# A graph-network layer on one core: rows of x fetched by SyncE and ScalarE's queue beside GpSimd's gathers, transfers moved to ScalarE's queue, copies moved to VectorE, shorter packing sums

## The chip, the cores and the metric

The kernel runs on one core of one Trainium2 chip. The metric is device time in microseconds (us); lower is better. A core has five engines that run side by side [...]: TensorE (PE, matrix products), VectorE (DVE), ScalarE (ACT), GpSimd (POOL) and SyncE (SP). SP, ACT and POOL each also have a queue from which they issue transfers (DMA) between the main memory (HBM) and the on-chip memory (SBUF); TensorE writes to a second on-chip memory, PSUM.

## The reference, cut to what matters

There are N = 50,000 nodes with D = 160 features and E = 1,650,000 edges (33 per node on average), sorted by destination; every node also has one edge from itself to itself.

```python
ss, vv = s[src], v[src]                       # one row of x per edge: the gather
out0 = C0 * (ss * e0 @ W1 + dot(vv, e1) * INV3 @ W2)
out1 = C1 * (p3 + p4 + p5)                    # all linear in x[src], scaled by the edge's 4 numbers
m_agg = segment_sum(concat(out0, out1), dst)  # sum over the edges of each node
h  = m_agg @ (Ws, Wv)                         # linear
x1 = layernorm(x + x + relu(h))
```

Everything before the relu is linear. So the kernel sums, for each node and each of the four edge numbers k, attr[e,k] * x[src[e]] over the node's edges, and applies one folded weight matrix per k afterwards.

## The kernel before, in words

**Units and groups.** The sorted edges are cut into units of 128 edges. Six units are a group (G = 6), and the destinations of a group lie within W = 32 consecutive nodes. There are 2,100 groups, taken two at a time (PG = 2) as a pair: 1,050 pairs of 12 units, 12,600 units in all. For a unit, GpSimd issues one indirect transfer (`gather`, L288) that reads 128 rows of x, 640 bytes each, into the tile `xg`, one per partition. VectorE builds the matrix `ha` (L297, L300) that puts each edge's four numbers in the columns of its destination; TensorE multiplies (`group_sums`, L325) and adds the six units of a group in PSUM. `xg` has six buffers (pool `rows`), `ha` three.

**Packing.** In the 1,980 middle groups a row is 787 edges long (L = 768 + 19), and self edges are taken out so that 768 remain. `pack` (L341) does this for 120 groups at once (17 packs): it loads source, destination and attributes (L351 to L354), marks the first 19 self edges of each row, sums their attributes by destination with 256 VectorE instructions (L389: 4 numbers, 32 destinations, two halves of the row), closes the gaps in steps of powers of two (L401 to L418), and stores the packed lists to HBM (L422, L423), from which `load` (L231) reads them back. The self edges' contribution is added when the group's sums leave PSUM (L334): it needs the 32 own rows of x, four times over, which `own` (L305) loads. For each pair `own` first reads two offsets from SBUF into SP's registers (L310) and then issues two transfers of 80 KB (L315); its pool has four buffers and it runs three pairs ahead.

**After the sums.** `turn` transposes the sums of two pairs (L436) and copies them out of PSUM (L439, the function `evict`), `apply_weights` multiplies by the folded weights (L450) and copies again (L454), `block` adds what belongs to 128 nodes (L480) and starts the layer norm, whose last step `norm3` (L188) stores the result (L192).

**Order.** The program is one long list, written by the loop over pairs at L595: load the next lists every ten pairs, gather, spread, sums, `own(p + 3)`, `fetch(p)`, some steps of `pack` (a generator; each `yield` is a place where it pauses, STEPS of them spread over the pairs), and then what `after_pair` has put off to this pair. Every engine and every queue works through its own instructions in that order. All loads and the packed stores are on SP's queue (`nc.sync`); the result's store is on ACT's (`nc.scalar`).

**The helper that is switched off.** `fetch` (L505), the plan of `batches` (L487 to L501) and the shortened `gather` (L287) can fetch whole units without GpSimd: an engine in `HELP` reads the offsets of some rows into registers (L510) and issues one transfer of 640 bytes for each row (L515). `HELP` (L63) is empty here, so none of it runs, and `evict` (L229) is ScalarE's copy.

Of the kernel before, what the change touches and what calls it, by code (L numbers as in the profile page):

```python
# [37 lines left out]
U8 = mybir.dt.uint8  # L38
# [24 lines left out]
HELP = {}  # L63
HEAD = 100
RP = 120
ROWS = 32
# [28 lines left out]
def tile_gnn_resnorm(ctx: ExitStack, tc: tile.TileContext, x, src, dst, attr, W1, W2, W3, W4, W5, Ws, Wv, out, n_edges):  # L95
# [92 lines left out]
    def norm3(pool, y, mv, rstd, n, row):  # L188
        nc.vector.reciprocal(rstd[:n], rstd[:n])  # L189
        o = pool.tile([P, D], F32, name="o")  # L190
        nc.vector.tensor_scalar(o[:n], y[:n], mv[:n, 0:1], rstd[:n], op0=ALU.subtract, op1=ALU.mult)  # L191
        nc.scalar.dma_start(out[row, :], o[:n])  # L192
# [18 lines left out]
    with tc.tile_pool(name="once", bufs=1) as once, tc.tile_pool(name="raw", bufs=2) as rawp, \  # L211
            tc.tile_pool(name="idx", bufs=2) as idxp, tc.tile_pool(name="rows", bufs=6) as rowp, \
            tc.tile_pool(name="far", bufs=3) as farp, tc.tile_pool(name="own", bufs=4) as ownp, \
# [13 lines left out]

        offsets = {}
        evict = nc.vector.tensor_copy if ET.Activation in HELP else nc.scalar.copy  # L229

        def load(s):  # L231
# [4 lines left out]
            if NH <= g0 < NH + NPK:  # L236
# [3 lines left out]
                for i in range(2):  # L240
                    nc.sync.dma_start(rf[:n, i, :], sd[i:i + 1, e].rearrange("o (u p) -> (o u) p", p=P))
                nc.sync.dma_start(ra[:n].rearrange("u p k -> u (p k)"), ad[e].rearrange("(u p) k -> u (p k)", p=P))
# [3 lines left out]
            nc.sync.dma_start(ri[:n, 0, :], src1[e].rearrange("(u p) o -> u (p o)", p=P))  # L246
            nc.sync.dma_start(ri[:n, 1, :], dst1[e].rearrange("(u p) o -> u (p o)", p=P))
            nc.sync.dma_start(ra[:n].rearrange("u p k -> u (p k)"), attr[e].rearrange("(u p) k -> u (p k)", p=P))
# [55 lines left out]

        def own(p):  # L305

            s, g, ng = pairs[p]
            if not NH <= g < NH + NPK:
                return
            _, at = nc.values_load_multi_w_load_instructions(  # L310
                baseO[0:1, g:g + ng], engines=[ET.SP], min_val=0, max_val=(N - W) * 4 * D,
                skip_runtime_bounds_check_because="an offset of a row of x")
            xo = ownp.tile([P, PG, D], F32, name="xo")
            for i, v in enumerate(at):
                nc.sync.dma_start(xo[:, i, :].bitcast(U8),  # L315
                                  xbytes[ds(v, W * 4 * D)].rearrange("(w f) -> w f", w=W).unsqueeze(0)
                                  .to_broadcast([NK, W, 4 * D]))
            owns[p] = xo
# [19 lines left out]
        owns, stored, taken = {}, {}, {}  # L338
        halves = ((0, L // 2), (L // 2, L))

        def pack(c):  # L341
# [9 lines left out]
            nc.sync.dma_start(pri[:n, 0, :], src1[e].rearrange("(r e) o -> r (e o)", e=L))  # L351
            nc.sync.dma_start(pri[:n, 1, :], dst1[e].rearrange("(r e) o -> r (e o)", e=L))
            nc.sync.dma_start(pra[:n].rearrange("r e k -> r (e k)"), attr[e].rearrange("(r e) k -> r (e k)", e=L))
            nc.sync.dma_start(pb[:n], base_d[NH + r0:NH + r0 + n])  # L354
            yield
            nc.scalar.copy(prs[:n], pri[:n])
# [3 lines left out]
            cum = packp.tile([P, L], F32, name="cum")  # L360
            far = packp.tile([P, L], I32, name="far")
            less = packp.tile([P, L], I32, name="less")
            carry = packp.tile([P, 1], F32, name="carry")
            pbf = packp.tile([P, 1], F32, name="pbf")
            mine = packp.tile([P, 2, NK * W], F32, name="mine")
            waste = packp.tile([P, L], BF16, name="waste")
            nc.vector.tensor_scalar(pbf[:n], pb[:n], float(N - W), None, op0=ALU.min)
            for h, (a, e) in enumerate(halves):
                q = slice(0, e - a)
                nc.vector.tensor_tensor(m[:, q], prs[:n, 0, a:e], prs[:n, 1, a:e], op=ALU.is_equal)  # L370
                nc.vector.tensor_tensor_scan(cum[:n, a:e], m[:, q], zeros[:n].to_broadcast([n, e - a]),
                                             carry[:n] if h else 0.0, op0=ALU.add, op1=ALU.add)
                nc.vector.tensor_copy(carry[:n], cum[:n, e - 1:e])
                yield

                nc.vector.scalar_tensor_tensor(m[:, q], cum[:n, a:e], float(K), m[:, q], op0=ALU.is_le, op1=ALU.mult)
                nc.vector.tensor_scalar(cum[:n, a:e], cum[:n, a:e], float(K), None, op0=ALU.min)
                nc.vector.scalar_tensor_tensor(far[:n, a:e], m[:, q], 0.0, cum[:n, a:e],
                                               op0=ALU.is_equal, op1=ALU.mult)
                yield  # L380
                nc.vector.tensor_scalar(cum[:n, a:e], prs[:n, 1, a:e], pbf[:n], None, op0=ALU.subtract)
                nc.vector.tensor_reduce(packed[:n, 0, 2 * c + h:2 * c + h + 1], cum[:n, a:e], axis=AX.X, op=ALU.min)
                nc.vector.tensor_reduce(packed[:n, 1, 2 * c + h:2 * c + h + 1], cum[:n, a:e], axis=AX.X, op=ALU.max)

                nc.vector.scalar_tensor_tensor(m[:, q], cum[:n, a:e], 1.0, m[:, q], op0=ALU.add, op1=ALU.mult)
                yield
                for k in range(NK):
                    for w in range(W):
                        nc.vector.scalar_tensor_tensor(waste[:n, a:e], m[:, q], float(w + 1), pra[:n, a:e, k],  # L389
                                                       op0=ALU.is_equal, op1=ALU.mult,  # L390
                                                       accum_out=mine[:n, h, k * W + w:k * W + w + 1])
                        if w % 4 == 3:
                            yield
            nc.vector.tensor_copy(counts[:n, c:c + 1], carry[:n])
# [426 lines left out]
```

## Time and profile before

| what | value |
|---|---|
| time, median of 3 runs | 18925.21 us (18899.5 to 18944.16) |
| the profiled execution's own time | 15879.8 us |
| its span, first to last instruction | 15878.0 us |
| GpSimd | 12,611 instructions, 75% of the span marked busy |
| TensorE products | 75% |
| VectorE | 50% |
| ScalarE | 6% |
| transfers, mean share of 16 DMA engines | about 0.3 in all slices |

The profile is of one execution. Its own time is 3045 us (16%) below the median of the timed runs, so durations from it are read as shares of its own span. "Busy" of GpSimd leaves out the time between two of its instructions, which is its own as well. SP's queue is not counted among the engines; what it issues is seen by asking for a line or for its waits.

### The profile page before, as it was taken

The page shows a single profiled execution, that of the slowest core. Times are in us where ns is not written, and L with a number is a line of the kernel's source. Part 1 is how long each engine was busy: PE and PEld are TensorE (multiplying, and loading weights), DVE is VectorE, ACT ScalarE, POOL GpSimd, SP SyncE. Part 2 cuts the span into 40 slices and gives each one's busy share as a digit, 9 for nine tenths or more (in the row PEclk, how much of TensorE's full clock was granted, in tenths as well). Part 3 has the DMA queues.
Part 4 walks back from the last instruction along what each step waited for, and adds up shares of the span by engine and source line. Part 5 has one row for each costly group of instructions (what it writes and reads, how often), then busy time and mean ns, then how long its engine had stood idle before and what let it go on. Part 6 is the DMA issues. An engine that isn't in the chain of part 4 may idle for free. (4 is left out here: it accounts for less than half of the span.)

```text
span 15878.0 us, 132047 instructions
## 1 busy us (share of the span) xinstructions
PE 11902.0 (75%) x43059; PEld 8781.1 (55%) x43060; DVE 7960.7 (50%) x17460; ACT 897.9 (6%) x2069; POOL 11926.1 (75%) x12611
## 2 busy tenths in 40 slices
PE   7677777777777777777777777777777777777777
PEld 4455555555555555555555555555555555555555
DVE  4565555545454554545454554545455454545422
ACT  0000000000000000000000000000000000000000
POOL 7677777777777777777777777777777777777776
PEclk7666666666666666666666666666666666666666
DMA  3333333333333333333333333333333333333332
GB/s 83 74 86 94 84 82 96 82 95 84 94 83 92 85 82 96 83 96 83 94 85 87 91 82 96 84 94 84 94 83 82 96 82 96 83 93 84 86 83 70
DMA packets 1040422, 1382.05 MB, mean 87 GB/s; under 512 B 233153, under 2 KB 813393, under 8 KB 1035641
## 3 DMA queue, kind: packets, MB, share of 16 engines
q0 software_dynamic: 604800, 1033.00, 26.9%
q1 hardware_dynamic: 378065, 307.98, 7.1%
q10 hardware_dynamic: 56864, 32.58, 0.7%
q8 instruction: 344, 5.64, 0.1%
q14 instruction: 349, 2.86, 0.1%
HBM read 1303.90 MB, written 68.75 MB: 86 GB/s over the span
## 5 line engine op out<-in xcount | busy, mean ns | idle before, releaser
L288 POOL DMA_INDIRECT xg<-in_x,si x12600 | 11924.5, 946 | 3917.0 <-issue 3527.0
L325 PE MATMUL ps<-xg,ha 128*128 128x160 f32 x25200 | 8037.7, 447 | 3686.5 <-DMA xg<-in_x,si 3640.6
L325 PEld LDWEIGHTS ps<-xg,ha 128*128 128x128 f32 x25200 | 5302.5, 266 | 6227.7 <-DMA xg<-in_x,si 6033.2
L334 DVE SCALAR_TENSOR_TENSOR A<-xo,taken,ps 128x160 f32<-128x160 f32 x1980 | 728.8, 377 | 7231.3 <-PE ps L325 7231.3
L389 DVE SCALAR_TENSOR_TENSOR waste<-marks,pra 120x393 bf16<-120x393 f32 (+3 forms) x4352 | 3652.5, 839 | 2.9
L300 DVE TENSOR_TENSOR ha<-hot,pk 128x1536 f32<-128x1536 f32 x1050 | 1830.2, 1744 | 284.1 <-PE ps L325 284.0
L480 PE MATMUL phb<-hp,hot 128*128 128x160 f32 x4544 | 1181.0, 433 | 56.2 <-ACT at L439 52.8
L480 PEld LDWEIGHTS phb<-hp,hot 128*128 128x128 f32 x4544 | 1066.4, 297 | 173.3 <-ACT at L439 172.2
L436 PE MATMUL pt<-ident,A 128*128 128x128 f32 (+1 forms) x4200 | 1051.7, 406 | 100.1 <-ACT hp L454 67.8
L450 PE MATMUL phc<-BWb,at 32*128 32x160 f32 x4200 | 1078.0, 404 | 0.0
L439 ACT COPY at<-pt 128x512 f32<-128x512 f32 (+1 forms) x1050 | 596.9, 579 | 6815.1 <-PE pt L436 6746.4
L450 PEld LDWEIGHTS phc<-BWb,at 32*128 32x128 f32 x4200 | 835.0, 253 | 196.3 <-issue 196.1
L450 PE MATMUL phc<-BWa,at 128*128 128x160 f32 x4200 | 922.6, 374 | 2.3 <-ACT at L439 2.0
L436 PEld LDWEIGHTS pt<-ident,A 128*128 128x128 f32 (+1 forms) x4200 | 700.7, 178 | 302.7 <-ACT hp L454 143.1
L450 PEld LDWEIGHTS phc<-BWa,at 128*128 128x128 f32 x4200 | 847.0, 255 | 35.3 <-ACT at L439 35.3
L297 DVE TENSOR_TENSOR hot<-bank,rel 128x384 f32<-128x384 f32 x1050 | 569.6, 544 | 0.3
L454 ACT COPY hp<-phc 128x160 f32<-128x160 f32 x525 | 153.3, 292 | 6230.2 <-PE phc L450 6171.5
L470 DVE TENSOR_TENSOR hot<-bank,rr 128x768 f32<-128x768 f32 (+2 forms) x391 | 358.8, 918 | 0.1
L389 DVE DVE_READ_ACCUMULATOR waste<-marks,pra 120x1 f32 (+1 forms) x4352 | 342.9, 79 | 0.0
L416 DVE COPY_PREDICATED pra<-marks,pra 120x1572 f32<-120x1572 int32 (+6 forms) x170 | 323.5, 1903 | 0.0
L176 DVE SCALAR_TENSOR_TENSOR y<-phb,xt 128x160 f32<-128x160 f32 x391 | 120.6, 308 | 195.6 <-PE phb L480 195.3
L414 DVE COPY_PREDICATED prs<-marks,prs 120x393 f32<-120x393 int32 (+6 forms) x340 | 181.3, 582 | 0.1
(98 smaller groups left out, 1610.1 us busy)
## 6 DMA issues: line engine op xcount, KB each, us to landing
xg<-in_x,si POOLq DMA_INDIRECT x12600
xo<-in_x SPq DMA_DIRECT2D x1980, 80.0 KB
xt<-in_x SPq DMA_DIRECT2D x390, 80.0 KB
out<-o ACTq DMA_DIRECT2D x390, 80.0 KB
ra<-ad SPq DMA_DIRECT2D x99, 240.0 KB
pra<-in_attr SPq DMA_DIRECT2D x16, 1475.6 KB
ad<-pra SPq DMA_DIRECT2D x16, 1440.0 KB
rf<-sd SPq DMA_DIRECT2D x198, 60.0 KB
```

The source lines that it names most:

```text
L288: nc.gpsimd.indirect_dma_start(out=xg[:, j, :], out_offset=None, in_=x, in_offset=bass.IndirectOffsetOnAxis(ap=placed[0][:, u + j:u + j + ...
L297: nc.vector.tensor_tensor(hot[:, :n], slotsP[:, 0:W].unsqueeze(1).to_broadcast([P, n, W]), rel[:, u:u + n].unsqueeze(2).to_broadcast([P, n ...
L300: nc.vector.tensor_tensor(ha[:, :n], hot[:, :n].unsqueeze(2).to_broadcast([P, n, NK, W]), pk[:, :, u:u + n].rearrange("p k u -> p u k").un ...
L325: nc.tensor.matmul(ps[:, j // G, :], ha[:, j].rearrange("p k w -> p (k w)"), xr, start=j % G == 0, stop=j % G == G - 1)
L334: nc.vector.scalar_tensor_tensor(A[:, i], xo[:, i], taken[r // RP][:, r % RP:r % RP + 1], ps[:, i], op0=ALU.mult, op1=ALU.add)
L389: nc.vector.scalar_tensor_tensor(waste[:n, a:e], m[:, q], float(w + 1), pra[:n, a:e, k], op0=ALU.is_equal, op1=ALU.mult, accum_out=mine[:n ...
L416: nc.vector.copy_predicated(pra[:n, a:e], mi[:, r].unsqueeze(2).to_broadcast([n, e - a, NK]), pra[:n, a + d:e + d])
L436: nc.tensor.transpose(pt[:f1 - f0, g, :], A[:, i, f0:f1], ident)
L439: evict(at[:, :, :ng].rearrange("f k g w -> f g k w"), pt[:f1 - f0, :ng].rearrange("f g (k w) -> f g k w", w=W))
L450: nc.tensor.matmul(ph[:ng * W], at[:, k, :ng].rearrange("f g w -> f (g w)"), bw[:, k, :], start=i == 0, stop=i == 2 * NK - 1)
L470: nc.vector.tensor_tensor(hot2[:, :len(cs)], slotsP.unsqueeze(1).to_broadcast([P, len(cs), P]), rr[:, :len(cs)].unsqueeze(2).to_broadcast( ...
L480: nc.tensor.matmul(ph[:nb], hot2[:r, i, :nb], hp[:r], start=i == 0, stop=i == len(cs) - 1)
```

## The change

- `HELP` becomes SP: 45 and ACT: 90. One unit in 45 is fetched by SP in four batches of 32 rows, one in 90 by ACT's queue in eight batches of 16 rows (`ROWS` by engine). Those units are left out of GpSimd's gathers.
- With ACT in `HELP`, `evict` becomes VectorE's copy, and `cast` also writes the byte offsets of all rows (L256 to L260).
- All other transfers move from SP's queue to ACT's (`dq = nc.scalar`). `own` reads the offsets of five pairs at once, with five buffers instead of four. The result's store is issued one pair after the work that makes it.
- In `pack`, the sums run only over the edges where a destination can lie (`degree`, `early`, `late`), 168 instructions a pack in place of 256; two more checks guard the assumption. Some instructions are merged or replaced; pauses are put between the loads and the cast and before the store.

```diff
-HELP = {}
+HELP = {ET.SP: 45, ET.Activation: 90}
-ROWS = 32
+ROWS = {ET.SP: 32, ET.Activation: 16}
...
-    def norm3(pool, y, mv, rstd, n, row):
+    def norm3(pool, y, mv, rstd, n):
...
-        nc.scalar.dma_start(out[row, :], o[:n])
+        return o
...
+        dq = nc.scalar
...
-                nc.sync.dma_start(ra[:n].rearrange("u p k -> u (p k)"), ad[e].rearrange("(u p) k -> u (p k)", p=P))
+                dq.dma_start(ra[:n].rearrange("u p k -> u (p k)"), ad[e].rearrange("(u p) k -> u (p k)", p=P))
...
+        OWN = 5
+
         def own(p):
...
-            _, at = nc.values_load_multi_w_load_instructions(
-                baseO[0:1, g:g + ng], engines=[ET.SP], min_val=0, max_val=(N - W) * 4 * D,
-                skip_runtime_bounds_check_because="an offset of a row of x")
+            if p % OWN == 0:
+                g1 = min(g + OWN * PG, NH + NPK)
+                _, at = nc.values_load_multi_w_load_instructions(
+                    baseO[0:1, g:g1], engines=[ET.Activation], min_val=0, max_val=(N - W) * 4 * D,
+                    skip_runtime_bounds_check_because="an offset of a row of x")
+                places.update(enumerate(at, g))
...
-            for i, v in enumerate(at):
-                nc.sync.dma_start(xo[:, i, :].bitcast(U8),
...
+            for i in range(ng):
+                dq.dma_start(xo[:, i, :].bitcast(U8),
...
+        degree = n_edges / N
+        late = 6 * math.sqrt(L) + 2 * degree
+        early = -6 * math.sqrt(L)
...
             yield
+            for _ in range(3):
+                yield
             nc.scalar.copy(prs[:n], pri[:n])
...
-                nc.vector.tensor_tensor(m[:, q], prs[:n, 0, a:e], prs[:n, 1, a:e], op=ALU.is_equal)
-                nc.vector.tensor_tensor_scan(cum[:n, a:e], m[:, q], zeros[:n].to_broadcast([n, e - a]),
-                                             carry[:n] if h else 0.0, op0=ALU.add, op1=ALU.add)
-                nc.vector.tensor_copy(carry[:n], cum[:n, e - 1:e])
+                nc.scalar.copy(m[:, q], prs[:n, 1, a:e])
+                nc.vector.tensor_tensor(m[:, q], prs[:n, 0, a:e], m[:, q], op=ALU.is_equal)
+                nc.vector.tensor_tensor_scan(cum[:n, a + 1:e + 1], m[:, q], most[:n].to_broadcast([n, e - a]),
+                                             cum[:n, a:a + 1], op0=ALU.add, op1=ALU.min)
...
-                for k in range(NK):
-                    for w in range(W):
-                        nc.vector.scalar_tensor_tensor(waste[:n, a:e], m[:, q], float(w + 1), pra[:n, a:e, k],
+                for w in range(W):
+                    w0 = max(a, math.floor(degree * w + early))
+                    w1 = min(e, math.ceil(degree * w + late) + 1)
+                    for k in range(NK if w0 < w1 else 0):
+                        nc.vector.scalar_tensor_tensor(waste[:n, w0:w1], m[:, w0 - a:w1 - a], float(w + 1), pra[:n, w0:w1, k],
                                                        op0=ALU.is_equal, op1=ALU.mult,
                                                        accum_out=mine[:n, h, k * W + w:k * W + w + 1])
...
-                        nc.vector.tensor_scalar(less[:n, a:e + d], far[:n, a:e + d], 0x7fffffff - d, None,
-                                                op0=ALU.bitwise_and)
+                        nc.vector.tensor_tensor(less[:n, a:e + d], far[:n, a:e + d], mi[:, 0:e + d - a],
+                                                op=ALU.subtract)
...
+            for _ in range(2):
+                yield
...
-                nc.sync.dma_start(sd[i:i + 1].rearrange("o (r e) -> (o r) e", e=G * P), prs[:n, i, :G * P])
-            nc.sync.dma_start(ad.rearrange("(r e) k -> r e k", e=G * P), pra[:n, :G * P])
+                dq.dma_start(sd[i:i + 1].rearrange("o (r e) -> (o r) e", e=G * P), prs[:n, i, :G * P])
+            dq.dma_start(ad.rearrange("(r e) k -> r e k", e=G * P), pra[:n, :G * P])
...
-            nc.sync.dma_start(xt[:nb], x[row, :])
+            dq.dma_start(xt[:nb], x[row, :])
...
+                nr = ROWS[eng]
                 _, at = nc.values_load_multi_w_load_instructions(
-                    offsets[s][u:u + 1, i * ROWS:(i + 1) * ROWS], engines=[eng], min_val=0, max_val=(N - 1) * 4 * D,
+                    offsets[s][u:u + 1, i * nr:(i + 1) * nr], engines=[eng], min_val=0, max_val=(N - 1) * 4 * D,
...
+        def do_send(b):
+            nb, row = rows_of(b)
+            dq.dma_start(out[row, :], outs.pop(b)[:nb])
...
                     after_pair(p + 6, do_store, b)
+                    after_pair(p + 7, do_send, b)
```

## The prediction

> **What bounds the kernel now.** I read the page's busy table and its costliest groups first, then the timeline of a stretch in the middle, then the lines that issue transfers.
>
> ```profile
> span 15878.0 us, 132047 instructions
> PE 11902.0 (75%) x43059; PEld 8781.1 (55%) x43060; DVE 7960.7 (50%) x17460; ACT 897.9 (6%) x2069; POOL 11926.1 (75%) x12611
> ...
> L288 POOL DMA_INDIRECT xg<-in_x,si x12600 | 11924.5, 946 | 3917.0 <-issue 3527.0
> ```
>
> GpSimd and TensorE show the same share. What separates them is what ended their idle time: of GpSimd's 3917 us, 3527 ended in "issue", which is its own next instruction. From the page's waits:
>
> ```profile
> PEld ps L325 <- DMA xg<-in_x,si: 6033.2, 7101, 8.5
> PE ps L325 <- DMA xg<-in_x,si: 3640.6, 6304, 8.1
> POOL xg L288 <- issue: 3527.0, 11578, 0.3
> POOL xg L288 <- PE ps L325: 196.2, 644, 0.3
> ```
>
> TensorE waits 3641 us for gathered rows, while GpSimd's wait for TensorE to give back a row buffer is never over 0.3 us. The timeline shows the beat:
>
> ```profile
> 8021.17 0.94 POOL L288 DMA_INDIRECT xg<-in_x,si  x1 [0.30 <-issue]
> 8022.42 0.95 POOL L288 DMA_INDIRECT xg<-in_x,si  x1 [0.30 <-issue]
> ```
>
> One unit every 1.25 us, busy 0.95 and 0.30 between. 12,600 x 1.25 = 15,750 of the span's 15,878; the other 128 us are head, tail and a few stretched beats. GpSimd's count of gathers is the time. VectorE (50%) and ScalarE (6%) are not in the way.
>
> Issuing a transfer costs its queue's engine time that the busy table leaves out. The lines of SP's queue, with minimum, median and maximum in ns:
>
> ```profile
> L310 SPq TENSOR_LOAD <-baseO x990: 640/975/3587, 46.0 to 15623.3; - x198
> L315 SPq MOVE xo<-in_x x1980: 29/38/38, 46.9 to 15637.6; - x198
> L315 SPq DMA_DIRECT2D xo<-in_x x1980: 547/585/708, 47.0 to 15637.7; - x198
> L466 SPq DMA_DIRECT2D xt<-in_x x391: 327/417/762, 23.1 to 15852.0; - x196
> L241 SPq DMA_DIRECT2D rf<-sd x198: 316/392/1723, 789.5 to 15172.1; - x198
> ```
>
> `xo` is the only transfer whose address comes from a register, as every row's will: 0.65 us each with its move and gaps (the timeline has two in 1.30 us). The others, with fixed addresses, take 0.32 to 0.42.
>
> [...] The trace shows the times only: 327 ns at the least for `xt` (128 partitions) and 316 for `rf` (120). [...] the transfer engines are about 0.3 busy, so room is there. [...] the trace has 640 to 975 ns for two. [...] The median here is 18,925.21 / 15,879.8 = 1.192 times the profiled execution; no run shows why, but [...] I scale by the ratio.
>
> **The change, part by part.**
>
> *Gathers removed.* Walking through the plan of batches with periods 45 and 90 gives 279 units for SP and 139 for ACT: 418 of 12,600. Saving 418 x 1.25 = 523 us; 15,878 - 523 = 15,355, a ratio of 0.967, or 18,302 us of timed run. The cover for the fetched rows is GpSimd's own gathering; if the rows are late, TensorE stands, then row buffers come back late (six pairs), and then GpSimd.
>
> *SP's new work.* 279 x 4 = 1,116 batches of 32 rows, one per 11.25 units; GpSimd needs 11.25 x (1 - 418/12,600) x 1.25 = 13.6 us for those. A batch is one register load of 32 offsets and 32 times (move, transfer, gaps), so 32c + T. T from below: 0.64 (no growth from two registers)[...]. I take 2. c from below: [...] 0.10 for move and gaps makes 0.27, an estimate; a bit less if a row is cheaper still. From above: `xo`'s 0.65. The limit is c = (13.6 - 2)/32 = 0.36. I take 0.27: `xo` names 128 pieces on a source with a repeated dimension, a row is one piece. Then 32 x 0.27 + 2 = 10.6 of 13.6 us. This is the step I am least sure of: the middle of the bounds, 0.46, is over the limit.
>
> *ACT's new work.* Per 11.25 units 16 rows (4.3), one register load (about 1), `xo` (2 x 0.65 = 1.3), offsets for five pairs (0.2), and `xt`, `out`, lists and packs, about one transfer of 0.4: 7.2 of 13.6 us. What stands behind them on ACT are the casts, the square root and the offsets' product; they feed steps pairs later. The pauses, the later store, five `own` buffers and the joint offset loads keep ACT from standing at a wait; I cost them at nothing, hidden by the other 6 us. Uncovered, one late store would hold all later loads, a few us at a time. SP's queue is freed of the 8763 us it stood waiting for `A` (L334) before an `xo`, which is why the row batches can flow there.
>
> *VectorE.* Out: 4352 sums x (839 + 79) ns = 3995 us. In: 17 x 168 = 2856 sums of on average 213 edges instead of 394, 839 x 213/394 = 454 ns plus 79 is 1522 us from below; with no saving per instruction 2622. I take 1700. Copies from ACT: 597 + 153 + 26 + 4 = 780 us by ACT's own rows. The merged and new instructions of the 17 packs are within 50 us either way. 7961 - 3995 + 1700 + 780 = about 6450 us, 42% of the new span. All of this is hidden behind GpSimd; with the cover gone it would be a gain of 1500 us on VectorE, and it isn't one here. A copy that now queues behind a 1.7 us `ha` product is late for TensorE by that much, and TensorE has 3 us to spare per pair.
>
> *Sum.* 15,355 plus some 25 us of beats stretched where a row comes late: 15,380, ratio 0.9685, 18,330 us.
>
> **Rivals.**
>
> *A: as above.* For: GpSimd's unbroken beat. Against: the price of a row is not in the trace. Own range 18,250 to 18,600.
>
> *B: SP's queue becomes the bound.* With c = 0.45, 32 x 0.45 + 2 = 16.4 us a batch, 1,116 batches = 18,300, and 50 us of head: 18,350 / 15,878 = 1.156, 21,900 us timed. It decides, as slower than before, from 15,878 / 1,116 = 14.2 us per batch, c = 0.38. For: `xo` at 0.65, and no transfer in the trace is issued under 0.31. Against: those have 100 pieces or more.
>
> *C: the two queues wait for each other.* SP's own waits have these:
>
> ```profile
> SPq L242 <- DMA xo<-in_x: 3.9, 3, 1.4
> SPq L248 <- DMA W<-in_L_gnn_W: 1.6, 1, 1.6
> ```
>
> A load of attributes has no use for `xo`, nor for a weight that ACT's queue fetched: transfers of both queues share a few completion semaphores in turn, and one waits until the earlier user has landed. With rows, 32 on SP and 16 on ACT stand in turn in the program, so ACT's wait for SP's last ones and SP's next for ACT's: at worst one after another, 48c per batch. At c = 0.39 that is 18.7 us, x 1,116 = 20,900, ratio 1.316, 24,900 us; it decides from 14.2/48, c = 0.296. At my c of 0.27 it would be 13.0 us, just hidden. Against: in 391 + 1980 transfers of before such waits make a few us; but they were few in flight.
>
> *D: no change.* c happens to lie near B's point of break-even, and the gain is given back: within 0.2% of 18,925.
>
> **How the numbers follow.** A change of 0.2% is about what a measurement can tell here. A 0.52, B 0.22, C 0.23, D 0.03. The range starts below A's full saving, 18,250, and must reach over A, D and B up to C's middle: of C about 0.13 and of B (c over 0.53) 0.05 lie above 25,000, so it ends there. A's own range stands above. Faster 0.52, same 0.03, slower 0.45.
>
> **What would show it.** Right: 12,182 gathers, still 1.25 us apart, with "issue" before them; rows issued by SP in under 0.3 us; `xo` waits gone from SP's queue; VectorE near 6450 us busy; TensorE hardly ever waiting for `xr`. Wrong by B: SP's queue issuing without a gap, TensorE's waits for the gathered rows turned into waits for `xr`, and GpSimd waiting for TensorE's `ps` for more than 0.3 us. Wrong by C: the same on TensorE and GpSimd, but SP and ACT each standing for long stretches at a landing of the other's rows. What makes the prediction wrong most easily is c.

## The result, and the profile after

| | before | after |
|---|---|---|
| time, median of 4 runs each, us | 18,915 (18,900 to 18,944) | 29,633 (29,575 to 29,687) |
| ratio | | 1.566, 95% interval 1.562 to 1.571 |
| span of the profiled execution, us | 15,878 | 29,573 |
| GpSimd's gathers | 12,600 | 12,182 |

The change makes the kernel slower by 57%. The forecast was 18,330 us, with a range to 25,000: it was wrong in sign, and the time lies above the range.

One sentence on the chips, without which the numbers below can't be read: the unchanged kernel takes 15,878 or 15,911 us on one of the five chips of the experiments (the profile of before shown above is of this kind) and 18,913 to 19,107 us on the four others (the timed runs of before, and the change, are of this kind), and every experiment is compared with the kernel before on its own chip.

The page of the changed kernel, the busy table and the groups that answer to those shown of before (busy time and mean ns, then the idle time just before, and what ended most of it):

```profile
span 29573.0 us, 235991 instructions
...
PE 8580.5 (29%) x43059; PEld 7539.0 (25%) x43060; DVE 7228.3 (24%) x16244; ACT 194.6 (1%) x556; POOL 11554.3 (39%) x12194
...
L291 POOL DMA_INDIRECT xg<-in_x,si x12182 | 11552.0, 948 | 17877.3 <-PE ps L333 7257.8
...
L333 PE MATMUL ps<-xr,ha 128*128 128x160 f32 x836 | 316.9, 475 | 14322.1 <-DMA xr<-in_x 14203.0
```

GpSimd's gathers still take 948 ns each, but its idle time rose from 3,917 to 17,877 us, and TensorE now stops it. TensorE stands 14,322 us ahead of 836 products with fetched rows. The waits say how long each time:

```profile
PE ps L333 <- DMA xr<-in_x: 14203.0, 277, 103.3
POOL xg L291 <- PE ps L333: 7257.8, 392, 89.7
POOL xg L291 <- PE pt L467: 6338.3, 161, 87.8
POOL xg L291 <- issue: 3471.1, 11361, 1.9
```

In the profile of before, GpSimd's wait for TensorE was never over 0.3 us; now one is up to 90 us. The chain runs from late rows (`xr`) to TensorE to GpSimd. That is what the prediction expected of TensorE and GpSimd under its rivals B and C alike; what tells them apart is whether SP issues without a gap or stands.

So the question is why SP's rows are late. For a row SP has two instructions: a MOVE of the row's address (ahead of the 829 transfers of SP in before whose addresses are fixed there is none) and DMA_DIRECT2D, the issue of the transfer. Their lines, in ns (minimum, median, maximum), and the largest of SP's waits:

```profile
L547 SPq MOVE xr<-in_x x35712: 1/29/1620, 11.1 to 29542.6; - x200
L547 SPq DMA_DIRECT2D xr<-in_x x35712: 1/208/1992, 19.8 to 29542.7; - x200
```

```profile
SPq L547 <- DMA xr<-in_x: 2431.1, 1654, 33.2
SPq L547 <- DMA xo<-in_x: 1075.7, 153, 55.2
SPq L547 <- DMA out<-o: 771.3, 120, 32.6
```

By their medians a row costs 0.24 us, and 0.30 to 0.34 with the gaps, a little over the forecast 0.27. But 29,573 / 1,116 = 26.5 us per batch, not 10.6. A timeline of two stretches, with SP's rows grouped and GpSimd's gathers around them, shows what the medians hide:

```profile
15067.86 22.20 SPq L547 DMA_DIRECT2D xr<-in_x  x43
15090.60 0.95 POOL L291 DMA_INDIRECT xg<-in_x,si  x1 [34.11 <-PE ps L333]
15091.85 0.95 POOL L291 DMA_INDIRECT xg<-in_x,si  x1 [0.31 <-issue]
...
15101.45 19.65 SPq L547 DMA_DIRECT2D xr<-in_x  x18
```

In the first stretch GpSimd stands (34.11 us), and SP issues 43 rows in 22.20 us. In the second GpSimd gathers every 1.25 us, but for one stand of 3.10 us, and SP issues 18 rows in 19.65 us. Register loads and long waits before rows are in both, 8.35 and 7.66 us; without them a row takes 0.32 us in the first and 0.67 in the second. Over the whole trace SP's instructions start 0.51 us apart on the mean while GpSimd gathers and about 0.2 us apart while it stands for long (gaps over 3 us left out). In the slow part a MOVE or an issue, 29 and 208 ns by their medians, often takes about 700 ns: 6,636 of SP's take 0.6 to 0.8 us, and after 4,427 of these at least one of the next two takes 15 ns or less. I call these the slow stretches.

In them SP and ACT go by a common beat. Of the neighbouring ends of long row instructions (0.6 to 0.8 us) of the two queues that are less than 1 us apart, 1,559 lie within 0.05 us of each other and 4,090 lie 0.66 to 0.74 us apart; none lies between. That would fit one thing that holds both queues in turn; no run shows what it is. Nothing points to the fetching of instructions: the page's queue "q14 instruction" moves 349 packets in before, 884 in e2 and 1,164 in the change; 12.1% of SP's long instructions start within 3 us after one of these, and 11.8% of the span lies there.

I split SP's time by kind, from the start and duration of every instruction on its queue and the completion semaphore that the trace names for each transfer. "Own" is instructions and gaps at full speed; "stretched" is transfers and MOVEs over 0.45 us and gaps of 0.3 to 0.8 us; "other queue" is standing over 0.8 us before a row whose completion semaphore (the trace has its updates by landing transfers) was last taken by a transfer of ACT's queue. In the change SP's 35,712 transfers and ACT's 21,002 use the same eight of these, each 7,089 or 7,090 times. In us per batch:

| run | own | stretched | other queue | other waits | span / batches |
|---|---|---|---|---|---|
| the change | 10.0 | 9.6 | 6.5 | 0.4 | 26.5 |
| SP alone (e2) | 10.4 | 7.6 | 8.3 | 0.2 | 26.5 |
| SP alone, one queue (e9) | 10.9 | 12.5 | 0.0 | 0.6 | 24.1 |
| SP alone, one gather in 12 (e13) | 12.0 | 0.7 | 3.8 | 0.0 | 16.6 |
| that, on one queue, chip of 15,878 us (e17) | 13.9 | 1.3 | 0.0 | 0.5 | 15.7 |
| the change's first half, chip of 15,911 us (e18) | 12.6 | 1.4 | 5.1 | 0.4 | 19.5 |

(On one queue "own" and "stretched" hold the 3,210 other transfers too; about 1 us of "stretched" there is the issue of `xo`, 0.55 us and more even when undisturbed. Rows issued in a slow stretch count under "stretched" whole, so "own" is too small where that is large.) The rest of the text is how the runs led to this table.

### The profile page after: what moved, and what is told of

Read it like the earlier page. It is cut to its first block, busy times and chain, and to the rows that moved or that the text cites. A ratio compares the mean times of both kernels' runs of the same rounds, so it can differ in the third digit from the quotient of the medians.

```text
span 29573.0 us, 235991 instructions
## 1 busy us (share of the span) xinstructions
PE 8580.5 (29%) x43059; PEld 7539.0 (25%) x43060; DVE 7228.3 (24%) x16244; ACT 194.6 (1%) x556; POOL 11554.3 (39%) x12194
## 3 DMA queue, kind: packets, MB, share of 16 engines
q1 hardware_dynamic: 71424, 23.00, 0.5%
q14 instruction: 1164, 9.53, 0.1%
## 5 line engine op out<-in xcount | busy, mean ns | idle before, releaser
L291 POOL DMA_INDIRECT xg<-in_x,si x12182 | 11552.0, 948 | 17877.3 <-PE ps L333 7257.8
L333 PE MATMUL ps<-xg,ha 128*128 128x160 f32 x24364 | 5425.9, 377 | 3793.4 <-issue 3563.0
L333 PEld LDWEIGHTS ps<-xg,ha 128*128 128x128 f32 x24364 | 4881.4, 254 | 4330.0 <-issue 4022.2
L333 PE MATMUL ps<-xr,ha 128*128 128x160 f32 x836 | 316.9, 475 | 14322.1 <-DMA xr<-in_x 14203.0
L418 DVE SCALAR_TENSOR_TENSOR waste<-marks,pra 120x236 bf16<-120x236 f32 (+45 forms) x2856 | 1497.4, 524 | 117.8 <-remote 13.8
L481 PE MATMUL phc<-BWb,at 32*128 32x160 f32 x4200 | 808.5, 315 | 421.4 <-issue 419.5
L470 DVE COPY at<-pt 128x512 f32<-128x512 f32 (+1 forms) x1050 | 670.9, 678 | 748.6 <-PE ps L333 362.2
L511 PE MATMUL phb<-hp,hot 128*128 128x160 f32 x4544 | 727.9, 312 | 10.9 <-issue 10.8
L511 PEld LDWEIGHTS phb<-hp,hot 128*128 128x128 f32 x4544 | 690.3, 203 | 12.8 <-issue 12.7
L481 PE MATMUL phc<-BWa,at 128*128 128x160 f32 x4200 | 665.4, 301 | 9.7 <-issue 9.4
```

The source lines that it names most:

```text
L291: nc.gpsimd.indirect_dma_start(out=xg[:, j, :], out_offset=None, in_=x, in_offset=bass.IndirectOffsetOnAxis(ap=placed[0][:, u + j:u + j + ...
L333: nc.tensor.matmul(ps[:, j // G, :], ha[:, j].rearrange("p k w -> p (k w)"), xr, start=j % G == 0, stop=j % G == G - 1)
L418: nc.vector.scalar_tensor_tensor(waste[:n, w0:w1], m[:, w0 - a:w1 - a], float(w + 1), pra[:n, w0:w1, k], op0=ALU.is_equal, op1=ALU.mult, a ...
L470: evict(at[:, :, :ng].rearrange("f k g w -> f g k w"), pt[:f1 - f0, :ng].rearrange("f g (k w) -> f g k w", w=W))
L481: nc.tensor.matmul(ph[:ng * W], at[:, k, :ng].rearrange("f g w -> f (g w)"), bw[:, k, :], start=i == 0, stop=i == 2 * NK - 1)
L511: nc.tensor.matmul(ph[:nb], hot2[:r, i, :nb], hp[:r], start=i == 0, stop=i == len(cs) - 1)
```

## The experiments

**e1: the helper switched off.** What is left is the moved transfers and the shorter packing.

```diff
-HELP = {ET.SP: 45, ET.Activation: 90}
+HELP = {}
```

> The changed kernel with HELP empty: no rows are fetched by SP or ACT, copies are back on ScalarE, all transfers stay on ACT's queue, the packing is the short one. In turn (rows of the two queues wait for each other), own price (SP's queue cannot issue 32 rows in time) and per row (each row costs the same wherever it is issued) all say: GpSimd makes 12,600 gathers again and the time is that of before, 18,900 us within 1%. Rival, that the moved transfers or the packing are what is slow: over 20,000 us.

Measured: 19,084 us, ratio 0.9995 (0.998 to 1.001). Moving the transfers and shortening the sums is worth nothing, as forecast; the whole loss comes with the helper, that is with the fetching or with the copies on VectorE that go with it.

**e2: SP alone.** Copies are on ScalarE again, since ACT isn't in `HELP`.

```diff
-HELP = {ET.SP: 45, ET.Activation: 90}
+HELP = {ET.SP: 45}
```

> The changed kernel with HELP holding SP: 45 alone; ACT's queue fetches no rows and ScalarE makes the copies. In turn: SP's 32 rows have nothing long to wait for, GpSimd sets the pace with 12,321 gathers, 18,915 x 0.978 = 18,500 us. Own price of SP's queue: as slow as the changed kernel, 29,600 us. Per row: two thirds of the excess stay, 18,500 + 0.667 x 11,300 = 26,000 us.

Measured: 29,593 us, 1.549 (1.546 to 1.552). As slow as the change: ACT's rows and the copies on VectorE are not needed for the loss.

**e3: SP's and ACT's rows in turn**, two to one in the program, instead of 32 and then 16.

```diff
-                for j, v in enumerate(at):
-                    r = i * nr + j
...
+                    todo += [((j + 0.5) / nr, eng, fetched[q, h], i * nr + j, v) for j, v in enumerate(at)]
+                for _, eng, xr, r, v in sorted(todo, key=lambda d: d[0]):
```

> The changed kernel with the same rows on the same queues, but in fetch the two queues' rows of a pair are issued in turn one by one (two of SP, one of ACT) instead of 32 of SP and then 16 of ACT. In turn: the two queues work side by side, a batch costs SP's 32 rows, some 13 us, close to GpSimd's 13.6, so 18,300 to 21,000 us. Own price and per row: 29,600 us as before.

Measured: 29,821 us, 1.561 (1.558 to 1.563). The order among the rows doesn't matter. At this point I took rival C, the waiting of the two queues for each other, for refuted. That was too quick, as e9 shows: e2 and e3 test the waits between rows and rows, not those between rows and ACT's other transfers.

**e4: ACT alone.**

```diff
-HELP = {ET.SP: 45, ET.Activation: 90}
+HELP = {ET.Activation: 90}
```

> The changed kernel with HELP holding ACT: 90 alone; copies on VectorE as in the change. In turn: ACT's 16 rows and its other transfers fit, 12,461 gathers, 18,915 x 0.989 = 18,700 us. Own price of SP's queue: also 18,700 us. Per row: a third of the excess stays, 18,700 + 0.333 x 11,300 = 22,500 us.

Measured: 20,833 us, 1.090 (1.088 to 1.092). Neither figure: 139 fetched units, all on one queue with the other transfers, cost 1,750 us.

**e5 to e8** take SP alone apart: half the batches, nobody reading, no registers, few transfers.

```diff
# e5
+HELP = {ET.SP: 90}
# e6: GpSimd gathers all units; the fetched rows are not used
+                          [fetched.pop((p, h)) for _, h in helped.get(p, [])][:0])
# e7: fixed addresses
+                    queues[eng].dma_start(xr[r:r + 1, :], x[k:k + 1, :])
# e8: one transfer of 32 rows
+                queues[eng].dma_start(xr[i * nr:(i + 1) * nr, :], x[k:k + nr, :])
```

> SP alone fetches rows, one unit in 90 (558 batches of 32 rows instead of 1,116; copies on ScalarE), all else as changed. Three theories of why SP's batch took 26.5 us (29,573 / 1,116) where 32 x 0.3 + 2.1 = 11.7 were its undisturbed price. "Fixed pace": SP needs about 26.5 us a batch whatever else runs, and it only shows where it is more than GpSimd's time: 558 x 26.5 = 14,800, hidden, so 19,084 (moved transfers alone) less 139 gathers x 1.25 to 1.5 = 18,870 to 18,910. "Shared": every batch takes its time from all engines, (29,593 - 19,084) / 1,116 = 9.4 us each, so 19,084 + 558 x 9.4 = 24,300. "Loop of waits": SP waits for TensorE to give back the row tile, TensorE for the rows, GpSimd for TensorE, and half as many units leave twice the time: 18,900 to 19,500.

> As SP alone at one unit in 45, but GpSimd gathers all 12,600 units and TensorE multiplies those; SP fetches its rows into the same tiles, and nobody reads them. Nobody waits for SP any more, and SP not for TensorE. "Fixed pace": the end is still SP's, 29,000 to 29,600, with GpSimd done near 19,100. "Shared": the end is slow too, and GpSimd's gathers are as stretched as before, done after 25,000. "Loop of waits": SP's batch falls to 12 to 16 us, 13,400 to 17,900 in all, and the end is GpSimd's, 19,100 to 19,600.

> As SP alone at one unit in 45, but each of the 35,712 rows is fetched from an address that is written in the instruction (so other rows of x than the edges', and other sums): no register loads, no MOVE ahead of each transfer. If the price lies in SP's count of instructions (a MOVE costs 0.7 us in the slow stretches as a transfer does), half the instructions go and the batch falls to about (26.5 - 2.1) / 2 = 12 us, 13,600 in all, hidden: 18,650 to 18,900. If it lies in the transfers (their issue and the waits for earlier ones to land), the batch is still 26.5 - 2.1 - 32 x 0.05 = 22.8 us: 25,400.

> As SP alone at one unit in 45, with the register loads of 32 offsets, but one transfer of 32 neighbouring rows at a fixed address in place of 32 of one row (so other rows of x than the edges'): 1,116 transfers instead of 35,712, the same 23 MB. Rows are the price: SP needs 1,116 x (2.15 + 0.4) = 2,850 us, hidden, and the 279 gathers fewer show: 19,084 - 279 x 1.25 to 1.5 = 18,670 to 18,740. If the register loads or TensorE's waiting for another queue's rows are the price: over 25,000. If fewer gathers don't shorten GpSimd's time: 19,050 to 19,150.

Measured: e5 23,072 us (1.220; 1.218 to 1.222), e6 31,493 (1.667; 1.659 to 1.674), e7 24,602 (1.301; 1.299 to 1.303), e8 19,010 (1.0045; 1.0029 to 1.0062).

In e5 half the batches cost 4,150 us, so SP doesn't have a fixed price of 26.5 us a batch. It comes nearest to "shared" (24,300).

e6 has no reader of the rows, and is slower still, at 28.1 us a batch. The waits of e6:

```profile
POOL xg L291 <- DVE rel L279: 13031.8, 100, 185.3
...
ACT ro L262 <- SPq L542: 8820.7, 87, 145.5
```

GpSimd now waits a hundred times, 130 us each, for the next list (`rel`). The list waits for ACT: its cast writes the offsets `ro` into one of two buffers, which SP must have read before (L542), and behind that cast ACT's queue holds all other transfers. With the readers gone, SP holds up the kernel through this buffer. The changed kernel has the same wait, 2,831 us in 95. The loop "SP waits for TensorE" falls, as SP is no faster.

e7 lies between its two figures, near the one for the transfers: without MOVE and register load 5,000 us go, but SP still stands 10,700 us for semaphores of ACT's transfers. In e8 the register loads, whose values were no longer used, were dropped from the program with the MOVEs, so its rows cost SP nearly nothing. It shows two things. The price goes away with the 35,712 MOVEs and all but 1,116 of as many transfers, though the bytes are the same. And the 279 gathers fewer bring nothing: the forecast step would have given 349 us, the run is 0.45% slower than before.

**e9 and e10: one queue.** All other transfers go back to SP, so that no two queues share a semaphore.

```diff
-        dq = nc.scalar
+        dq = nc.sync
...
-                    baseO[0:1, g:g1], engines=[ET.Activation], min_val=0, max_val=(N - W) * 4 * D,
+                    baseO[0:1, g:g1], engines=[ET.SP], min_val=0, max_val=(N - W) * 4 * D,
```

> SP alone fetches rows (one unit in 45), and all other transfers are issued by SP too, ahead of and between the rows (in the change they are on ScalarE's queue). In the trace of SP alone, 9,238 of the 9,340 us that SP stood for more than 0.8 us before a row were on a completion semaphore last taken by a transfer of ScalarE's queue, 102 on one of SP's own. "Shared turns": the two queues take eight completion semaphores in turn, so that each waits for the other's transfers to be issued and to land, and they go in step; on one queue that is gone, and SP's time is its own instructions, 11,400 us, the excess in slow stretches, up to 7,700, and 3,210 transfers x 0.5 = 1,600: 19,000 to 21,500. "Number of instructions" (each of SP's 72,900 instructions takes 0.14 us from a supply that all engines share) or "price of a row": 29,500 to 31,500, as both counts are the same or higher.

> The same with one unit in 90: 558 batches, all transfers on SP. On two queues this took 23,072. "Shared turns": SP has 5,100 us of row instructions, up to 6,000 in slow stretches and 1,600 of others, hidden: 18,700 to 19,400. "Number of instructions" or "price of a row": 23,000 or more.

Measured: e9 26,891 us, 1.411 (1.409 to 1.414), where two queues took 1.549; e10 20,831 us, 1.093 (1.091 to 1.095), where two took 1.220. The waits for the other queue went from 8.3 us a batch to none: they were the shared semaphores', as the trace of e2 had put them down. But the gain is 2,700 us in e9, not the 8,000 or more that was expected, and 2,200 in e10, not 3,700 or more: in e9 the stretched part grew from 7.6 to 12.5, of which about 1 is the issue of `xo`. "Shared turns" is one cause and not the larger one. e10 is as slow as e4, with as many rows, on another engine and with the copies elsewhere: so e4's 9% isn't the copies'.

**e11: instructions without transfers.** e8, with the register load of 32 offsets back in and 64 register instructions in each batch.

```diff
+                for j in range(6 * nr):
+                    nc.sync.reg_mul(tick, tick, 3)
+                    nc.sync.reg_add(tick, tick, 1)
                 queues[eng].dma_start(xr[i * nr:(i + 1) * nr, :], x[k:k + nr, :])
```

(The 384 operations are built as 64 instructions.)

> Blocks of 32 neighbouring rows in one transfer (1,116 transfers, as in the run with blocks, 19,010), but with the register load of 32 offsets and 64 register instructions of arithmetic in each batch, so that SP has about 75,000 instructions, as in the change, and no more transfers. "Shared turns" and "price of a row": 18,950 to 19,300. "Number of instructions": 28,000 to 30,000, with stretches of 0.7 us an instruction.

Measured: 23,170 us, 1.216 (1.214 to 1.218): 4,160 more than e8, with not one transfer more. It misses both figures. The register instructions, in ns, and TensorE's wait:

```profile
L550 SPq FUSED_REGOPS  x71424: 1/74/1642, 14.2 to 23092.3; - x200
```

```profile
PE ps L333 <- DMA xr<-in_x: 7148.8, 230, 46.1
```

SP is the bound again: the 1,116 register loads take 2,034 us, and the rest is mostly arithmetic, 74 ns apiece by the median but over 0.6 us for 9,449 of them. So slow stretches need no row transfers. Of instructions started while GpSimd had stood for more than 8 us, under 1 in 100 came 0.6 to 0.8 us after the one before; while it gathered, 16 to 30 in 100. That made the gathers the suspect.

**e12: the kernel before, a second profile.**

> The kernel before, unchanged, for a second profile: its first one shows 15,878 where its timed runs take 18,921. If the timed runs hold pauses that the first profile lacks, this one shows about 18,900, GpSimd's gathers 1.25 us apart but for a pause of 4 to 5 us once in 24 gathers (12,600 / 24 x 5 = 2,600 to 3,000 us in all), as the profile with HELP switched off shows. If not, 15,880 and no pauses.

Measured: 19,098 us, and the pauses are there: 760 beats of GpSimd are over 1.3 us and take 3,283 us more than 1.25 us each, against 92 with 85 us in the profile shown of before. From its timeline:

```profile
8037.38 0.95 POOL L288 DMA_INDIRECT xg<-in_x,si  x1 [0.30 <-issue]
8043.66 0.94 POOL L288 DMA_INDIRECT xg<-in_x,si  x1 [5.33 <-PE ps L325]
```

and its row of `xo`, whose MOVE had a maximum of 38 ns in the first profile:

```profile
L315 SPq MOVE xo<-in_x x1980: 3/38/1442, 48.2 to 18876.3; - x198
```

213 MOVEs take over 600 ns. So the timed executions of before hold the same slow stretches, TensorE falls behind in them, and about once in 20 gathers (616 times) GpSimd stands some 5 us. That is the 19% by which the median lies above the first profile, and it is why e8 gained nothing there: GpSimd's beat is not unbroken on these chips.

**e13 to e15: fewer gathers.** GpSimd gathers one unit in 12 (e13; e14 with `HELP` off), or every second (e15), and TensorE takes those rows for the others.

```diff
# e13 (e14 with HELP = {}; e15 with 2 for 12)
-            for j in range(n - len(others)):
+            for j in range(0, n - len(others), 12):
...
-            return [xg[:, j, :] for j in range(n - len(others))] + others
+            return [xg[:, j // 12 * 12, :] for j in range(n - len(others))] + others
```

> SP alone at one unit in 45, on two queues (29,593), but GpSimd gathers only the first unit of each pair and TensorE multiplies those rows for the others too (other sums; one gather in 12 is left, 1,050). In the traces so far SP's instructions start 0.45 to 0.53 us apart while GpSimd gathers and 0.15 to 0.23 while it stands. "Beside the gathers" (an instruction of SP is dear only while GpSimd gathers): SP's 72,900 instructions take 0.2 us each, 14,600, with little standing still: 13,000 to 17,000. "SP's own price" (dear because of its own transfers or their number, whatever GpSimd does): 25,000 to 29,600.

> HELP switched off (19,084) and the same single gather in 12: the floor of the other engines. If TensorE and the chain behind it set the time once gathers are gone: 9,500 to 13,500, and no pauses; if the pauses of 4 to 5 us per 24 units have nothing to do with gathers, 525 of them stay: 12,500 to 16,000.

> As with few gathers, but every second unit is gathered (about 6,300). "Beside the gathers": GpSimd runs for 6,300 x 1.25 to 1.45 = 7,900 to 9,100, in which SP issues 17,000 to 20,000 instructions, and the other 53,000 to 56,000 take 0.2 to 0.25: 19,000 to 23,000 in all. "SP's own price": 26,000 to 29,600.

Measured: e13 18,566 us (0.981; 0.973 to 0.990), e15 21,932 (1.159; 1.149 to 1.169), e14 6,322 (0.334). SP's lines of e13:

```profile
L547 SPq MOVE xr<-in_x x35712: 3/29/426, 10.9 to 18466.6; - x200
L547 SPq DMA_DIRECT2D xr<-in_x x35712: 3/208/1960, 18.5 to 18466.7; - x200
```

The longest MOVE is 426 ns, and there are no slow stretches. SP's batch falls from 26.5 to 16.6 us, for the same 35,712 rows, and with half the gathers it is 19.6, with 879 MOVEs over 0.6 us. On these chips the slow stretches need the gathers, by their issuing or by their traffic; "SP's own price" falls. e13 is above its figure by the wait for the other queue that is left:

```profile
SPq L547 <- DMA xo<-in_x: 3059.3, 1432, 58.6
```

e14, with no helper, shows about how long the other engines need, far below what I expected: a third of the kernel's time.

**e16: the same bytes without GpSimd.**

```diff
+            nc.scalar.dma_start(xg[:, :m, :], x[k:k + P * m, :].rearrange("(j p) f -> p j f", p=P))
```

> SP alone at one unit in 45, two queues, and no gathers at all: the units' rows come as one plain transfer per pair on ScalarE's queue, of neighbouring rows of x, in 1,536 pieces of 640 bytes (other sums), so that as many bytes in pieces as long as the gathers' arrive without GpSimd. "GpSimd's issuing" slows SP: no stretches of 0.7 us, a MOVE takes 29 ns nearly everywhere, SP's instructions 0.2 us apart, and the total is near that with few gathers, 17,000 to 22,000, more by what SP waits for the new transfers. "The traffic" of the gathers slows SP: 15 to 20 in 100 of SP's instructions are 0.6 to 0.8 us apart while the rows arrive, and the total is 24,000 to 30,000.

**e17: few gathers on one queue**: the edits of e13 and e9 together.

> One gather in 12 (18,566 on two queues, 16.6 us a batch), with all transfers on SP. The first of these had 13,500 us in SP's own instructions and 4,800 us before rows, 4,226 of them for a transfer of ScalarE's queue on the same semaphore. If that wait is the shared semaphores' doing, it goes, and 3,210 transfers x 0.5 come: 13,500 + 1,600 = 15,100, so 14,500 to 16,000. If SP waits for something else: 18,000 to 20,000.

Measured: e16 20,336 us (1.281; 1.270 to 1.291), e17 17,561 (1.106; 1.103 to 1.109). These two ran on the chip where the kernel before takes 15,878. There no kernel shows the stretches (in before, e16, e17 and e18 no MOVE of SP's transfers is over 38 ns), so e16 can't tell issuing from traffic. e17 shows that with one queue SP hardly waits before its rows any more:

```profile
SPq L323 <- DVE mv L181: 219.6, 22, 28.5
```

It is the largest of its waits, and not one for a landing. The batch is 15.7 us, of which the 3,210 other transfers are about 1.5: above the 14,500 to 16,000 expected, as the register loads and the issue take 0.2 us and 17 ns more each than in e13.

**e18: the change in the first half, plain loads in the second.**

```diff
+            if plain:
+                k = (u * 4099) % (N - P * PG * G)
+                nc.scalar.dma_start(xg[:, :m, :], x[k:k + P * m, :].rearrange("(j p) f -> p j f", p=P))
...
+                          [fetched.pop((p, h)) for _, h in helped.get(p, [])], p >= 525)
```

> The change itself for the first 525 pairs; for the last 525, no gathers, but one plain transfer per pair on ScalarE's queue, of neighbouring rows in pieces of 640 bytes (other sums there), so that the bytes still arrive. The last call ran on a chip on which the kernel before takes 15,878 and no kernel shows stretches of 0.7 us, so its run with plain transfers could not tell GpSimd's issuing from the traffic; both halves of one run can, on either kind of chip. Where the kernel before takes 18,900 to 19,100: first half 14,500 to 15,000 with stretches of 0.7 us (half of 29,600); second half, if GpSimd's issuing makes them, none and 9,000 to 12,000, and if the traffic makes them, as many and over 13,000. Where it takes 15,878: no stretches in either half, and the first half shows the change without them: if the rows would then be hidden, as the prediction had it, 7,700 to 7,900; if SP still waits 4 us and more a batch for the other queue's transfers, 558 batches x 16.6 to 18 = 9,300 to 10,000.

Measured: 22,222 us in all, on the chip of 15,911. The two halves (the last gather starts at 10,748 us): their length, then the busy time of the products, of the weight loads and of the gathers with `xg`, the granted clock, the share of the DMA engines and GB/s:

```profile
0.00:10748.00 10748.00, 2003.56 (x12092) 1905.82 (x12092) 5778.38 (x6092) 0.64 0.26 65
10748.00:22163.00 11415.00, 1999.99 (x12272) 1920.54 (x12272) 0.00 (x0) 0.64 0.22 60
```

and SP's rows:

```profile
L552 SPq MOVE xr<-in_x x35712: 29/29/38, 10.7 to 22136.6; - x200
L552 SPq DMA_DIRECT2D xr<-in_x x35712: 207/208/1993, 16.7 to 22136.6; - x200
```

No MOVE is over 38 ns, and no row is issued in under 207 ns. Without any slow stretch the change's half still takes 10,748 us, above the 9,300 to 10,000 expected, against 15,911 / 2 = 7,955 of before: 35% slower. Of its 19.5 us a batch, 12.6 are SP's own, and 5.1 are waits for transfers of ACT's queue. So the change would have lost on this kind of chip too, by the shared semaphores together with a price of a row that leaves no room for them.

No version here that fetches every row that it needs beats the kernel before.

## Why the prediction was wrong

**The step that failed** is "SP's new work": "32 x 0.27 + 2 = 10.6 of 13.6 us". The prices in it were my estimates, and somewhat too low: 0.27 us a row, of which 0.10 for move and gaps, left 0.17 for the issue, about half of the least in the trace of before (316 ns); it measured 0.208 (median). Without stretches, in e13, a row costs (7,438 + 149 + 1,073 + 2,370) / 35,712 = 0.31 us (transfers, MOVEs, small gaps) where I chose 0.27, and a load of 32 registers 2.15 us where I chose 2; that makes 12.1 us, still under 13.6 but with half the room (e18, on the other kind of chip, has 12.6). The sum failed because two terms are missing in it.

- **The other queue.** "C: the two queues wait for each other" had the cause of this wait: in before the two queues' 3,210 transfers take eight completion semaphores, 401 or 402 each, and in the change too they share eight. I put it down to rows against rows alone, "48c per batch", and weighed it by how few such waits before had. (The sum also left out the register loads: with 2 us, c = 0.27 gives 15.0 us and not 13.0, over the limit.) In the change ACT's rows are about half of it, 3,660 of 7,220 us. The other half are ACT's `xo`, `xt`, lists and results, which stand in ACT's queue behind casts and copies and their waits; without rows on ACT (e2) they alone hold SP 9,240 us. Standing before a row whose semaphore such a transfer took last is 4 to 8 us a batch in the runs of the table on two queues, and there is none on one (e9, e17). The 13.6 us have no room for it. Before, the loads stood on one queue beside ACT's few stores, so the trace had hardly a case to show.
- **What GpSimd does meanwhile.** I took a queue's time as a price per instruction, whatever else runs. On the chips with slow stretches SP's instructions beside all gathers start 0.44 to 0.53 us apart (the change, e2, e3, e5, e6, e9), and 0.2 to 0.25 while GpSimd stands for over 3 us. SP then falls behind, TensorE stands for `xr`, GpSimd for TensorE, and only while it stands does SP catch up. In e2, with GpSimd's stands of over 3 us taken out, its running time is 15,470 us, and SP issues 23,200 of its 72,900 instructions in it; the other 49,700 take 14,110 us more. e13 and e15 show that the gathers are needed for this, though not by what way; the first profile of before, with no MOVE over 38 ns, could not.

**The scaling.** "I scale by the ratio", 1.192, took it that all queues run slower alike in the timed runs. That was my assumption, and the traces speak against it. The granted TensorE clock is 0.648 in the profile of before at 15,878 us and 0.665 in the one at 19,096 us. GpSimd's gather takes the same 0.95 us in both. The ratio was itself the sign of the stretches: timed runs that take 19% more than the profile contain something that the profile lacks.

**"Gathers removed"**, 418 x 1.25 = 523 us: not realised. e8, with 279 fewer and cheap rows, gained nothing (19,010 us, 0.45% slower). On the chips of 18.9 ms GpSimd's count is not the time. On the chip of 15.9 ms it wasn't tried with cheap rows.

**"ACT's new work"** costed the waits on ACT "at nothing". The offsets' two buffers make ACT stand for SP, 2,831 us in the change, and e6 shows that the kernel can be held up through them.

**What held.** e1: moving the transfers and the shorter sums are worth nothing. The shorter sums themselves take 1,497 + 235 = 1,732 us on VectorE for the 1,700 forecast. The copies take 913 us there instead of 780, and all durations together fell by 1,256 us where 1,515 were forecast. The busy time fell less, to 7,228 us instead of 6,450, since fewer of these durations overlap in the record (768 us of them, 1,291 before); all of it is hidden. The register load takes 2.15 us for 32 (median of SP's 1,116 in the change), or 67 ns a register; the 2 us of the forecast were my estimate.

**The rivals.** B had its signs on TensorE and GpSimd right, and its time too low (21,900); but it wanted SP to issue without a gap, by a dearer row of 0.45 us, and SP stands 6.5 us a batch. C was in part right: it had the standing for the other queue, and the same signs on TensorE and GpSimd. Neither had the slow stretches. The range ended at 25,000, because I counted the dearest case as one cause at a time.

**What stays open.** Why some chips have the stretches and one has not; and whether GpSimd's issuing or the gathers' traffic makes them: both runs meant for that fell on the chip without them. The stretches go with the chips used here, but each chip served for a short time only, so a state that passes isn't excluded. Nor was it tested whether the recording of the executions has a part: in the change 4,353 of SP's 35,712 issues of rows are recorded at under 50 ns, where e18 has none under 207, so the recorded times in a stretch can't all be the time of the work itself, and the executions of every experiment have recorded spans.

## What to carry to other kernels

A queue that is to work beside a saturated engine needs ample room before it is called hidden: here a batch of 12.1 us undisturbed took 26.5 us, and 19.5 on the chip without slow stretches. Its waits must be counted through the completion semaphores that it shares with another queue as well (6.5 us a batch in the change), not only through its data. Small transfers on one queue and late, waiting transfers on another did not run independently here (8.3 us of standing a batch in e2): keep them on one queue (e9, 2,700 us less), or make the small ones few (e8, 0.45% slower than before). Where the timed runs are a fifth above the profiled execution, find out what the profile lacks before scaling by the ratio.

## What the runs showed of the hardware that was not expected

- MOVEs of 29 ns and issues of 208 ns often take about 700 ns in the slow stretches, beside GpSimd's gathers on four of five chips, and where SP and ACT both fetch rows, their long instructions end together or 0.66 to 0.74 us apart; with one gather in 12 left, no MOVE is over 426 ns.
- Register instructions of SP, 71,424 of arithmetic and 1,116 loads, with no more transfers, cost the kernel 4,160 us (e11 against e8).
- Issuing a row of 640 bytes takes 208 ns on SP and 234 on ACT, beside 316 and more for the transfers to 120 and 128 partitions in before (`rf`, `xt`).
- With one gather in 12 left and no helper the kernel needs 6,322 us, at a granted TensorE clock of 0.991 and TensorE 96% busy:

```profile
PE 6059.2 (96%) x43059; PEld 5765.3 (91%) x43060; DVE 5940.4 (94%) x14592; ACT 872.5 (14%) x2103; POOL 997.9 (16%) x1062
```

  e13, with the same products and TensorE 36% busy, was granted 0.668.
